# Layer 1's convolution as sums over tap rows by even and odd image rows

## The chip, the cores and the metric

The kernel runs on one core of one Trainium2 chip. A core has five engines with an instruction queue each: TensorE (PE; its weight loads are listed as PEld), VectorE (DVE), ScalarE (ACT), GpSimd (POOL) and SyncE (SP), which here only issues DMAs. Each engine works through its own queue in order; semaphores tie the queues together. The metric is the device time of one execution in microseconds, the median of several runs. One execution is also recorded by the hardware profiler; its trace is what is called the profile here.

## The reference: a hybrid of four layers

The input is x of 2 x 256 channels x 32 x 32, float32. Layer 0 is two Mamba blocks with normalisation, layer 1 a convolution with attention over a neighbourhood, layers 2 and 3 attention with experts. The change concerns layer 1:

```python
def _L1_conv_ref(x, w1, b1, w2, b2):
    k = lax.conv_general_dilated(x, w1, window_strides=(1, 1),
            padding=[(6, 6), (6, 6)], rhs_dilation=(2, 2), ...) + b1
    k = lax.conv_general_dilated(k, w2, ...) + b2          # 1x1, to 49 channels
    attn = softmax(k, axis=1)
    xp = pad(x, 6 on each side of both image axes)
    shifts = stack([xp[:, :, 2*u : 2*u + H, 2*v : 2*v + W] for u in 7 for v in 7])
    return einsum('bkchw,bkhw->bchw', shifts, attn)
```

So for each pixel 49 logits come from a 7 x 7 convolution with taps two pixels apart (tap row u and tap column v), followed by a 1 x 1 convolution; their softmax weighs the 49 shifted copies of x. Layer 0 ahead of it gives the x.

In layer 0 a Mamba block runs, for every image, 512 inner channels and 16 states n, the recurrence h = da * h + du * B along the 1024 pixels, and sums h * C over n.

## The kernel before

*Merged taps.* The 1 x 1 convolution follows the 7 x 7 one with nothing between, so the kernel multiplies the two weights once: `Taps.make` (from line 914) gives 7 x 7 taps of 256 channels x 49 outputs. It runs in 28 parts (tap row u, four of the 14 blocks "v, channel half" at a time), two steps each: PE transposes of w1 (`w1t`, line 939), an ACT copy, PE products with w2 (`taps_ps`, line 945), an ACT copy `taps_sb` (line 950), and a DMA of it on SP to a buffer in HBM. These steps are placed in the scans of layer 0, by `paced` (line 743): it hands out the steps of a list between given slots of a unit of scans, one slot for each scan.

*Layer 0's scans.* A unit of work is a chunk of 512 pixels of one image in one block: 2 images x 2 chunks x 2 blocks are eight units (`Mamba.scan`, line 546). In a unit, for each n = 0 to 15: SP loads `m_b` (line 599, four buffers), POOL makes m_h = m_du * m_b in two halves of 128 x 1024 (line 607, in the trace under the helper's line 179; six buffers), ACT the exponential m_da (line 617), VectorE four scans in place in m_h (line 621), PE transposes the result into `m_ht` (lines 575 and 577), and VectorE (line 591, `m_ya`) or ACT (line 589, `m_s`) multiplies it with C and gathers. Beside this the next unit's input products, `m_conv`, `m_delta`, `m_du` and so on are worked off in the slots. POOL's elementwise operations go through `Net.lined` (line 174), which chains each to the one before, so POOL works them off in the order in which the program emits them. The other engines' instructions are ordered by a scheduler.

*The convolution.* Sixteen output rows of 32 pixels fill one PSUM bank (512 float32 a partition). `Taps.convolve` (line 987) makes four passes, u = 3, 0, 1, 2; a pass takes tap rows u and u + 4 side by side as a weight block of 98 outputs (`Taps.load`, line 971; for u = 3, which has no partner, POOL sets the other half to zero). Since tap row u + 4 belongs to image rows eight below, the sums of both halves are kept eight (in pixels of one row phase: four) rows apart, in 35 rows over three banks, and the shift is undone when the logits of the 98 partitions are added, by two small products (line 1110). For each of seven v, two channel halves and each bank: one matmul of up to 512 columns, line 1001. 154 of them make an image; in the trace each float32 matmul is two instructions, so 308. `Taps.read` (line 1009) takes the banks with one ACT and one VectorE operation each into `lg`.

*Where it runs.* Image 0 (`early` in `layer0`, from line 861): two banks' steps lie in the slots of the last unit of layer 0 (slots 3 to 63), the third bank's follow its scans, beside layer 0's last products and norm. Image 1 (`layer1`, line 1031): `both` (line 757) takes two steps of the convolution and then one of a chain: turning image 0 (`turn`), weighing it (`weigh`: softmax, the band matrices, line 1126 on, and their products), and turning image 1.

Of the kernel before, what the change touches and what calls it, by code (L numbers as in the profile page):

```python
# [10 lines left out]
F32 = mybir.dt.float32  # L11
# [8 lines left out]
P = 128  # L20
NB = 2
HW = 1024
W = 32
# [742 lines left out]
def layer0(net, x, x_dram, m1, m2, load_image, taps, conv_dram, lg):  # L766
# [5 lines left out]
    with (  # L772
# [45 lines left out]
        for u, (m, j) in enumerate(units):  # L818
# [38 lines left out]
            if u + 1 < len(units):  # L857
                more = not u
                for n, first, end in ((2, 12, 32), (4, 35, 47), (3, 58, 63)):
                    steps += [(islice(aside, n + more), n + more, first, end)]  # L860
            else:
                last.close()
                m.ps_da = last.enter_context(tc.tile_pool(name="m_da2", bufs=2, space=PSUM))
                ps_acc = last.enter_context(tc.tile_pool(name="m_acc", bufs=1, space=PSUM))

                def place(u):
                    pool, tag, w = {
                        3: (one, "pre", TC + 3), 0: (two, "xs", TC), 1: (two, "delta", TC),
                        2: (two, "du", TC),
                    }[u]  # L870
                    a = pool.tile(
                        [P, NDC, w], F32, tag=tag, name=f"early_{u}",
                        bufs=3 if tag == "xs" else None,
                    )
                    return taps.load(u, a.rearrange("p d t -> p (d t)"))

                pair = {u: place(u) for u in taps.ORDER}
                def early():
                    for k in range(2):
                        a = ps_acc.tile([P, TC], F32, tag="acc", name=f"early_acc{k}")  # L880
                        acc = {k: taps.bank(a)}
                        yield from taps.convolve(0, pair, acc)
                        taps.read(acc, lg)

                steps += [(early(), 112, 3, 63)]
            own = m.back(j, u + 1 == len(units), u + 2 < len(units))
            if u + 1 == len(units):

# [5 lines left out]
        for _ in islice(done[0], 2):  # L894
            pass
        net.line = None
        acc = {2: taps.bank(ps_ht.tile([P, TC], F32, tag="ht", name="early_acc2"))}
        both(taps.convolve(0, pair, acc), done[0], 3)
        taps.read(acc, lg)


class Taps:
# [3 lines left out]
    def __init__(self, net, pool, keep, x, w1, w2):  # L906
# [4 lines left out]
        self.w2_sb = pool.tile([P, NTAP], F32, tag="w2", name="w2_sb", bufs=1)  # L911
        nc.scalar.dma_start(self.w2_sb, w2)

    def make(self, psum, dram):

        net, nc, pool = self.net, self.net.nc, self.pool
        self.made = [dram.tile([P, 14, NTAP], F32, name=f"taps_{u}") for u in range(7)]
        parts = [(u, k) for u in range(7) for k in range(0, 14, 4)]
        loaded = []

        def load():
# [5 lines left out]
            )  # L927
            loaded.append(w)

        load()  # L930
        load()
        for i, (u, k) in enumerate(parts):
            if len(loaded) < len(parts):
                load()
            w = loaded[i]
            n = min(4, 14 - k)
            ps = psum.tile([P, TC], F32, tag="mm", name=f"w1t_{u}_{k}")
            for a in range(n):
                nc.tensor.transpose(ps[:, a * P : (a + 1) * P], w[:, a, :], net.ident)
            wt = pool.tile([P, TC], F32, tag="w1t", name=f"w1ts_{u}_{k}", bufs=1)  # L940
            nc.scalar.copy(wt[:, : n * P], ps[:, : n * P])
            yield
            ps = psum.tile([P, TC], F32, tag="mm", name=f"taps_ps_{u}_{k}")
            for a in range(n):
                nc.tensor.matmul(
                    ps[:, a * NTAP : (a + 1) * NTAP], lhsT=wt[:, a * P : (a + 1) * P],
                    rhs=self.w2_sb, start=True, stop=True,
                )
            out = pool.tile([P, 4, NTAP], F32, tag="taps", name=f"taps_sb_{u}_{k}", bufs=3)
            nc.scalar.copy(  # L950
                out[:, :n, :], ps[:, : n * NTAP].rearrange("p (i t) -> p i t", t=NTAP)
            )
            nc.sync.dma_start(self.made[u][:, k : k + n, :], out[:, :n, :])
            yield


# [9 lines left out]
        nc.vector.tensor_copy(self.bias[:NTAP, :], ps[:NTAP, 0:1])  # L966
        yield

    ORDER = (3, 0, 1, 2)

    def load(self, u, flat):

        nc = self.net.nc
        w = flat[:, : 28 * NTAP].rearrange("p (a k t) -> p a k t", k=2, t=NTAP)
        if u == 3:
            nc.gpsimd.memset(w[:, :, 1, :], 0.0)
        for k in range(2):
            if u + 4 * k < 7:
                nc.sync.dma_start(w[:, :, k, :], self.made[u + 4 * k])
        return w.rearrange("p a k t -> p a (k t)")  # L980

    @staticmethod
    def bank(tile):

        return tile[: 2 * NTAP, :].rearrange("p (r c) -> p r c", c=W)

    def convolve(self, b, pair, acc):

        nc = self.net.nc
        for u in self.ORDER:  # L990
            r0 = 6 - 2 * u

            for v in (3, 0, 1, 2, 4, 5, 6):
                ci, co = max(0, 2 * v - 6), max(0, 6 - 2 * v)
                n = W - abs(2 * v - 6)
                for kc in range(NCC):
                    lhsT = pair[u][:, v * NCC + kc, :]
                    for k, a in acc.items():
                        lo, hi = max(16 * k, r0), min(16 * k + 16, r0 + W)
                        if lo < hi:  # L1000
                            nc.tensor.matmul(  # L1001
                                a[:, lo - 16 * k : hi - 16 * k, co : co + n], lhsT=lhsT,
                                rhs=self.x[:, kc, b, lo - r0 : hi - r0, ci : ci + n],
                                start=(u == (0 if k == 2 else 3) and v == 3 and kc == 0),
                                stop=(u == 2 and v == 6 and kc == NCC - 1),
                            )
                    yield

    def read(self, acc, lg):

        nc = self.net.nc
        for k, bank in acc.items():
            rows = 3 if k == 2 else 8
            src = bank.rearrange("m (r a) (h c) -> m a r c h", a=2, c=2)
            for a in range(2):
                to, at = lg[:, a, 8 * k : 8 * k + rows], src[:, a, :rows]
                if a:
                    nc.vector.tensor_scalar_add(to, at, self.bias)  # L1018
                else:
                    nc.scalar.activation(to, at, AF.Identity, bias=self.bias)  # L1020
            if k == 2:
                nc.gpsimd.memset(lg[:, :, 19], 0.0)

    @staticmethod
    def logits(tile):
        return tile[: 2 * NTAP, : 40 * W].rearrange(
            "m (a r c h) -> m a r c h", a=2, r=20, c=2
        )


def layer1(ctx, net, x, t, taps, lg0):
# [12 lines left out]
    one = ctx.enter_context(tc.tile_pool(name="c_one", bufs=1, side="right"))  # L1044
    two = ctx.enter_context(tc.tile_pool(name="c_two", bufs=2, side="right"))
    with (
        tc.tile_pool(name="c_pair", bufs=4) as pairs,
        tc.tile_pool(name="c_acc", bufs=1, space=PSUM) as ps_acc,
        tc.tile_pool(name="c_ps", bufs=1, space=PSUM) as ps2,
    ):  # L1050
        pair = {
            u: taps.load(u, pairs.tile([P, 28 * NTAP], F32, tag="pair", name=f"pair_{u}"))
            for u in taps.ORDER
        }
        lg, xk = {0: lg0}, {}

        def convolve(b):
            acc = {
                k: taps.bank(ps_acc.tile([P, TC], F32, tag=f"acc{k}", name=f"acc{k}"))
                for k in range(3)  # L1060
            }
            yield from taps.convolve(b, pair, acc)
            lg[b] = taps.logits(taps.keep.tile([P, 40 * W], F32, tag="lg", name=f"lg{b}"))
            taps.read(acc, lg[b])
            yield

        eye = one.tile([P, H + 6], F32, name="eye")
        nc.vector.memset(eye, 0.0)  # L1070
# [32 lines left out]
        def weigh(b, psum, tag):  # L1103

            att = one.tile([P, per, NTAP], F32, name=f"att{b}")
            for q in range(per):
                ps = psum.tile([P, TC], F32, tag=tag, name=f"lg_{b}_{q}", bufs=2)
                for k in range(2):
                    r = q % 4 * 4 + 4 * k
                    nc.tensor.matmul(  # L1110
                        ps[:, :NTAP],
                        lhsT=lg[b][:, q // 4, r : r + 4].rearrange("m r c h -> m (r c h)"),
                        rhs=net.ident[: 2 * NTAP, k * NTAP : (k + 1) * NTAP],
                        start=(k == 0), stop=(k == 1),
                    )
                nc.vector.tensor_copy(att[:, q, :], ps[:, :NTAP])
                if q % 4 == 3:
                    yield
# [46 lines left out]
                nc.vector.tensor_copy(t[:, b * per + q, :], ops[:, :C])  # L1165
            yield

        both(convolve(1), chain(turn(0), weigh(0, ps2, "a"), turn(1)), 2)
    return lambda psum, tag: weigh(1, psum, tag)


# [969 lines left out]
def conv_attn_hybrid(ctx: ExitStack, tc: tile.TileContext, a: dict, out: bass.AP):  # L2141
    nc = tc.nc
    net = Net(ctx, tc, a["cols"], a["rows"])
    main = ctx.enter_context(tc.tile_pool(name="main", bufs=1))
    lg = Taps.logits(main.tile([P, 40 * W], F32, tag="lg", name="lg0"))
    image = ExitStack()
    x = image.enter_context(tc.tile_pool(name="image", bufs=1, side="right")).tile(
        [P, NCC, NB, HW], F32, name="x"
# [159 lines left out]
```

## Time and profile before

| | us |
|---|---|
| median of 3 runs | 2045.58 |
| lowest and highest | 2043.87 and 2050.39 |
| profiled execution | 2050.42 |
| its span | 2048.7 |
| mean granted clock of TensorE | 0.961 |

The time splits so (bounds of the units found from the first scan of each):

| stretch | from | to | length |
|---|---|---|---|
| units 1 to 6 of layer 0's scans (unit 0 is first) | 165.5 | 876.8 | 711.3 |
| unit 7, with image 0's convolution | 876.8 | 1014.3 | 137.5 |
| layer 0's end | 1014.3 | 1056.2 | 41.9 |
| image 1's convolution in layer 1 | 1056.2 | 1165.5 | 109.3 |
| the rest: weighing of image 1, layers 2 and 3 | 1165.5 | 2048.7 | 883.2 |

How to read the rows: a group's row gives line, engine, operation, output and input tiles (names without numbers), shapes and count; then the busy time, the mean duration of one in ns; then the idle time of the engine just before them with what ended most of it. A row of windows gives the busy time and count on PE, PEld, VectorE, ScalarE and POOL, the granted clock (1.00 is full speed), the DMA share and GB/s. A row of the timeline gives start, length, engine, line, operation, tiles and how many were merged, in brackets what the engine waited for. Over the whole span the engines are busy like this:

```profile
PE 1874.6 (92%) x9938; PEld 1344.7 (66%) x9938; DVE 1332.1 (65%) x2138; ACT 946.9 (46%) x1713; POOL 1074.4 (52%) x729
```

The parts of `make` lie in units 0 to 5 (the copies from 86.0 to 751.8) and touch, in the trace, line 945's PE row (196 products, 26.9 us) and line 950's ACT row (28 copies, mean 0.32 us for the wide ones).

### The profile page before, as it was taken

The page shows a single profiled execution, that of the slowest core. Times are in us where ns is not written, and L with a number is a line of the kernel's source. Part 1 is how long each engine was busy: PE and PEld are TensorE (multiplying, and loading weights), DVE is VectorE, ACT ScalarE, POOL GpSimd, SP SyncE. Part 2 cuts the span into 40 slices and gives each one's busy share as a digit, 9 for nine tenths or more (in the row PEclk, how much of TensorE's full clock was granted, in tenths as well). Part 3 has the DMA queues.
Part 4 walks back from the last instruction along what each step waited for, and adds up shares of the span by engine and source line. Part 5 has one row for each costly group of instructions (what it writes and reads, how often), then busy time and mean ns, then how long its engine had stood idle before and what let it go on. Part 6 is the DMA issues. An engine that isn't in the chain of part 4 may idle for free. (4 is left out here: it accounts for less than half of the span.)

```text
span 2048.7 us, 27882 instructions
## 1 busy us (share of the span) xinstructions
PE 1874.6 (92%) x9938; PEld 1344.7 (66%) x9938; DVE 1332.1 (65%) x2138; ACT 946.9 (46%) x1713; POOL 1074.4 (52%) x729
## 2 busy tenths in 40 slices
PE   8788988988898988899999989999999899999995
PEld 3355665656565665655666555568999666799994
DVE  5889898998989989898614285774222445652223
ACT  4777877777877767674302253322111122221111
POOL 7788896978979698975404250012333200033330
PEclk9889999999999999799999999999999999999997
DMA  4334344343435334362130100046999400359995
GB/s 150 97 91 116 87 122 135 78 122 82 132 90 141 82 86 111 86 140 63 31 57 1 52 0 1 32 186 247 326 322 332 168 21 21 142 197 320 328 324 186
DMA packets 98857, 271.78 MB, mean 133 GB/s; under 512 B 35916, under 2 KB 54225, under 8 KB 82325
## 3 DMA queue, kind: packets, MB, share of 16 engines
q1 hardware_dynamic: 81268, 198.03, 29.1%
q0 software_dynamic: 14432, 68.31, 13.5%
q10 hardware_dynamic: 3008, 3.55, 0.5%
q8 instruction: 83, 1.36, 0.3%
q14 instruction: 66, 0.53, 0.1%
HBM read 200.80 MB, written 22.77 MB: 109 GB/s over the span
## 5 line engine op out<-in xcount | busy, mean ns | idle before, releaser
L179 POOL TENSOR_TENSOR m_h<-m_du,m_b 128x1024 f32<-128x1024 f32 x253 | 602.8, 2471 | 149.8 <-PE m_ht L577 73.5
L617 ACT ACTIVATE m_da<-m_delta,m_aneg 128x512 f32<-128x512 f32 x512 | 349.2, 694 | 153.2 <-DVE m_h L621 144.1
L621 DVE TENSOR_TENSOR_SCAN m_h<-m_da,m_state,m_h 128x512 f32<-128x512 f32 x256 | 314.0, 1266 | 22.0 <-POOL m_h L179 13.6
L577 PEld LDWEIGHTS m_ht<-ident,m_h 128*128 128x128 f32 x1600 | 193.5, 146 | 193.3 <-issue 64.2
L621 DVE TENSOR_TENSOR_SCAN m_h<-m_da,m_h 128x512 f32<-128x512 f32 x256 | 299.3, 1205 | 21.6 <-ACT m_da L617 16.5
L577 PE MATMUL m_ht<-ident,m_h 128*128 128x128 f32 x1600 | 254.1, 286 | 59.5 <-DVE m_h L621 28.4
L591 DVE SCALAR_TENSOR_TENSOR m_ya<-m_ht,m_ct,m_ya 128x512 f32<-128x512 f32 x324 | 231.3, 732 | 58.6 <-PE m_ht L577 49.6
L2067 PEld LDWEIGHTS h<-xts,we_l_late 128*128 128x128 f32 x2048 | 239.0, 193 | 10.6 <-issue 6.0
L2067 PE MATMUL h<-xts,we_l_late 128*128 128x128 f32 x2048 | 241.3, 276 | 4.6 <-DMA we_l_late<-in_l_experts_dram 1.9
L2075 DVE TENSOR_TENSOR hid<-hid,h 128x512 f32<-128x512 f32 x79 | 54.2, 686 | 236.6 <-PE h L2067 232.5
L1806 POOL DMA_INDIRECT x_l_early<-l_zs,l_source x15 | 17.8, 1187 | 339.1 <-ACT pt L1570 138.6
L2074 ACT ACTIVATE hid<-h 128x512 f32<-128x512 f32 x79 | 47.1, 597 | 315.7 <-PE h L2067 315.7
L575 PE MATMUL m_ht<-ident,m_h 128*128 128x128 f32 x896 | 140.5, 306 | 29.5 <-ACT m_s L589 13.4
L575 PEld LDWEIGHTS m_ht<-ident,m_h 128*128 128x128 f32 x896 | 124.3, 212 | 52.5 <-DVE m_h L621 16.8
L1806 POOL DMA_INDIRECT x_l_late<-l_zd,source x64 | 65.4, 1023 | 149.4 <-PE xt L2050 145.3
L2082 PE MATMUL o<-we_l_late,hid 128*128 128x256 f32 x512 | 122.7, 381 | 4.1 <-DVE y L2087 2.8
L430 PE MATMUL m_conv<-m_pre,m_taps 128*128 128x512 f32 x240 | 117.7, 609 | 5.8 <-ACT m_xs L436 3.4
L2089 POOL DMA_INDIRECT l_yd<-y,target x64 | 65.4, 1022 | 106.3 <-DVE y L2087 94.4
L589 ACT ACTIVATE m_s<-m_ht,m_ct 128x512 f32<-128x512 f32 x156 | 104.5, 686 | 31.8 <-DMA m_yb<-m_s 15.8
L2082 PEld LDWEIGHTS o<-we_l_late,hid 128*128 128x128 f32 x512 | 91.8, 190 | 15.3 <-DVE y L2087 3.9
L1001 PE MATMUL early_acc<-x,early 128*98 128x448 f32 (+24 forms) x308 | 98.6, 446 | 0.4 <-DVE lg L1018 0.4
L1001 PE MATMUL acc<-x,pair 128*98 128x416 f32 (+21 forms) x308 | 94.6, 455 | 0.0
(412 smaller groups left out, 3128.0 us busy)
## 6 DMA issues: line engine op xcount, KB each, us to landing
we_l_late<-in_l_experts_dram SPq DMA_DIRECT2D x64, 1536.0 KB, 9.5
m_yb<-m_s POOLq DMA_DIRECT2D x39, 1024.0 KB, 8.5
m_b<-m_bd SPq DMA_DIRECT2D x128, 256.0 KB, 3.5
we_l_early<-in_l_experts_dram SPq DMA_DIRECT2D x15, 1536.0 KB, 8.2
m_ya<-m_yb POOLq DMA_DIRECT2D x7, 1024.0 KB, 8.8
w<-in_l_w_dram SPq DMA_DIRECT2D x21, 256.0 KB, 6.1
l_yl<-l_yd SPq DMA_DIRECT2D x8, 512.0 KB, 10.7
l_zd<-l_z SPq DMA_DIRECT2D x7, 512.0 KB, 3.3
```

The costliest lines, as they stand in the source:

```text
L179: self.line = do(*args, **named)
L430: nc.tensor.matmul(ps, lhsT=self.taps[:, dc * 4 + k, :], rhs=pre[:, dc, k : k + TC], start=(k == 0), stop=(k == 3),)
L575: nc.tensor.matmul(a, lhsT=h, rhs=net.ident, start=True, stop=True)
L577: nc.tensor.transpose(a, h, net.ident)
L589: nc.scalar.activation(to[:, i, :], ps, AF.Copy, scale=c)
L591: nc.vector.scalar_tensor_tensor(ya[:, i, :], ps, c, ya[:, i, :], ALU.mult, ALU.add)
L617: net.decayed = nc.scalar.activation(da, delta[:, dc, :], AF.Exp, scale=self.aneg[:, i : i + 1])
L621: nc.vector.tensor_tensor_scan(h, da, h, 0.0 if first else state[:, n, dc : dc + 1], ALU.mult, ALU.add)
L1001: nc.tensor.matmul(a[:, lo - 16 * k : hi - 16 * k, co : co + n], lhsT=lhsT, rhs=self.x[:, kc, b, lo - r0 : hi - r0, ci : ci + n], start=(u ...
L1806: nc.gpsimd.indirect_dma_start(out=x, out_offset=None, in_=rows[:, :], in_offset=bass.IndirectOffsetOnAxis(ap=source[:, g : g + 1], axis=0 ...
L2067: nc.tensor.matmul(ps[:, at], lhsT=w12[:, s, kc, at], rhs=xt[:, kc * P : (kc + 1) * P], start=(kc == 0), stop=(kc == NCC - 1),)
L2082: gate.o = nc.tensor.matmul(ps[:, :C], lhsT=ht[:, mc * P : (mc + 1) * P], rhs=w[:, 8 + mc, :], start=(mc == 0), stop=(mc == NHC - 1),)
```

## The change

With taps two rows apart, an output row of one row phase reads input rows of the same phase only. Call s the row pair within a phase's even or odd half: the rows of a phase are split once more into even ones and odd ones. The seven tap rows are then a filter of odd and even taps over even and odd rows, a filter of length 7 over two half-rate sequences. The change computes it with three sums, a scheme in which one sum is shared by both halves:

- sum 0 runs on (even + odd rows added, the new tile `both`, made by POOL in two 128 x 512 additions) with tap rows 3, 1 and 5;
- sum 1 runs on odd rows with the tap differences 6-5, 4-3, 2-1 and 0;
- sum 2 runs on even rows with 2-3, 0-1, 6 and 4-5;
- even output rows are sum 0 + sum 1, odd ones sum 0 + sum 2 (with the bias in sums 1 and 2).

Each sum covers half the image's rows, so it fits one bank. There are 113 matmuls an image instead of 154; a sum goes through 28 or 29 steps and its bank is then read: sums 1 and 2 by one ACT and one VectorE operation, sum 0 by four VectorE additions into `lg`.

What else moves:
- `make` has 24 new POOL subtractions (`less`, through `lined`), one after each part with u > 0, from two neighbouring copies; one buffer. Its parts run with u as the inner loop. SP writes 44 pieces instead of 28, of 196 bytes per block where two are side by side.
- The taps are kept in pairs (a to f) and loaded with 6 contiguous loads instead of 7; the zero half is gone.
- In `layer0`: the early pairs lie in other buffers (d, c, e, f; a and b together in "pre"), the three early sums share one bank one after the other, 67 of the 87 steps lie in slots 5 to 63 and the last 20 after the scans, one to each step of layer 0's end.
- In `layer1`: three steps of the convolution to one of the chain; all tap pairs have a buffer of their own; `lg` has 36 instead of 40 rows.

The core of the diff:

```diff
+    PAIRS = {
+        "a": ("3", "1"), "b": ("5",), "c": ("6-5", "4-3"), "d": ("2-1", "0"),
+        "e": ("2-3", "0-1"), "f": ("6", "4-5"),
+    }
+    SUMS = (
+        (1, (("d", -1, 1, 8, 0), ("c", 0, 0, 1, 1), ("c", 1, 0, 7, 0))),
+        (2, (("e", 0, 0, 8, 0), ("f", 1, 0, 1, 1), ("f", 2, 0, 6, 0))),
+        (0, (("a", 0, 0, 8, 0), ("b", 1, 0, 7, 0))),
+    )
+    STEPS = 3 * (7 * NCC * 2 + 1)
...
-        parts = [(u, k) for u in range(7) for k in range(0, 14, 4)]
+        parts = [(u, k) for k in range(0, 14, 4) for u in range(7)]
...
+        def keep(name, tile, k, n):
+            if name in home:
+                pair, i = home[name]
+                nc.sync.dma_start(self.made[pair][:, k : k + n, i, :], tile[:, :n, :])
...
-            nc.sync.dma_start(self.made[u][:, k : k + n, :], out[:, :n, :])
+            keep(f"{u}", out, k, n)
+            if u:
+                less = pool.tile([P, 4, NTAP], F32, tag="less", name=f"less_{u}_{k}", bufs=1)
+                x, y = (past, out) if u % 2 else (out, past)
+                net.lined(nc.gpsimd.tensor_sub, less[:, :n, :], x[:, :n, :], y[:, :n, :])
+                keep(f"{u - 1}-{u}" if u % 2 else f"{u}-{u - 1}", less, k, n)
             yield
...
+    def added(self, b, both):
+        rows = self.x[:, :, b].rearrange("p k (s e a) w -> p k e s a w", e=2, a=2)
+        for kc in range(NCC):
+            self.net.lined(
+                self.net.nc.gpsimd.tensor_add, both[:, kc],
+                rows[:, kc, 0], rows[:, kc, 1],
+            )
+    def convolve(self, b, pair, both, bank, lg):
         nc = self.net.nc
+        rows = self.x[:, :, b].rearrange("p k (s e a) w -> p k e s a w", e=2, a=2)
+        for which, passes in self.SUMS:
+            acc = bank(which)
+            if which == 2:
+                self.added(b, both)
+            src = both if which == 0 else rows[:, :, which % 2]
             for v in (3, 0, 1, 2, 4, 5, 6):
                 ci, co = max(0, 2 * v - 6), max(0, 6 - 2 * v)
                 n = W - abs(2 * v - 6)
                 for kc in range(NCC):
+                    first = v == 3 and kc == 0
+                    todo = list(passes if which or first else passes[::-1])
+                    if first and which == 1:
+                        todo[1:] = ("c", 1, 0, 1, 0), ("c", 1, 1, 7, 0), passes[1]
+                    for i, (name, rho, lo, hi, edge) in enumerate(todo):
+                        w = pair[name][:, v * NCC + kc]
+                        w = w[:, 1, :] if edge else w.rearrange("p k t -> p (k t)")
+                        nc.tensor.matmul(
+                            acc[: w.shape[1], lo:hi, :, co : co + n], lhsT=w,
+                            rhs=src[:, kc, lo + rho : hi + rho, :, ci : ci + n],
+                            start=first and i == 0,
+                            stop=v == 6 and kc == NCC - 1 and i + 1 == len(todo),
+                        )
+                        if i in (0, len(todo) - 1):
+                            yield
+            self.read(which, acc, lg)
+            yield
...
-                steps += [(early(), 112, 3, 63)]
+                early = early()
+                many = Taps.STEPS - 20
+                steps += [(islice(early, many), many, 5, 63)]
...
-        acc = {2: taps.bank(ps_ht.tile([P, TC], F32, tag="ht", name="early_acc2"))}
-        both(taps.convolve(0, pair, acc), done[0], 3)
-        taps.read(acc, lg)
+        both(early, done[0], 1)
...
-        both(convolve(1), chain(turn(0), weigh(0, ps2, "a"), turn(1)), 2)
+        both(convolve(1), chain(turn(0), weigh(0, ps2, "a"), turn(1)), 3)
```

## The prediction

> **What bounds the kernel now.** I read the page first (busy shares and slices), then the windows of layer 0's units and of layer 1, then the timeline of the stretches the change touches. One execution was profiled: 2050.42 us, of which 2048.7 are the span, so 1.7 lie around it; it stands 4.8 above the median of 2045.58. All sums below are made against 2050.4 and carried to the median at the end. A shift of 0.3%, 6 us, is about the least a measurement of this kernel can tell from none.
>
> From the page:
> ```profile
> L179 POOL TENSOR_TENSOR m_h<-m_du,m_b 128x1024 f32<-128x1024 f32 x253 | 602.8, 2471 | 149.8 <-PE m_ht L577 73.5
> L621 DVE TENSOR_TENSOR_SCAN m_h<-m_da,m_state,m_h 128x512 f32<-128x512 f32 x256 | 314.0, 1266 | 22.0 <-POOL m_h L179 13.6
> L1001 PE MATMUL early_acc<-x,early 128*98 128x448 f32 (+24 forms) x308 | 98.6, 446 | 0.4 <-DVE lg L1018 0.4
> L1001 PE MATMUL acc<-x,pair 128*98 128x416 f32 (+21 forms) x308 | 94.6, 455 | 0.0
> ```
> The convolution (line 1001) is some 95 us of TensorE per image. In the scans, POOL's m_h idles 149.8 us, half of it for m_ht to free its buffers: POOL runs ahead of VectorE, whose scans wait for POOL only 13.6 us here. That lead is what the change spends.
>
> Windows (PE, PEld, DVE, ACT, POOL busy; granted clock): two ordinary units of layer 0, the last unit with image 0's convolution, its tail, and layer 1:
> ```profile
> 282.20:399.80 117.60, 104.16 (x541) 69.45 (x542) 105.81 (x120) 93.40 (x172) 98.84 (x50) 0.97 0.44 118
> 399.80:517.30 117.50, 105.07 (x541) 71.50 (x539) 107.24 (x119) 89.52 (x142) 100.67 (x51) 0.96 0.41 102
> 876.80:1014.30 137.50, 133.53 (x571) 77.57 (x570) 109.16 (x121) 71.59 (x106) 83.32 (x44) 1.00 0.35 80
> 1014.30:1056.20 41.90, 39.55 (x245) 30.78 (x243) 13.43 (x43) 5.00 (x13) 7.47 (x23) 0.98 0.17 32
> 1056.20:1165.50 109.30, 107.43 (x419) 61.32 (x419) 29.44 (x62) 19.56 (x56) 36.63 (x57) 0.98 0.10 15
> ```
> An ordinary unit is VectorE's (106-107 of 117.5 us), with PE and POOL close behind. The last unit is TensorE's: 133.5 of 137.5, 20 us longer than the others with no more VectorE work. Layer 1 is TensorE's too, 107.4 of 109.3. In the last unit even POOL waits for the transposes (timeline):
> ```profile
> 984.45 4.65 POOL L179 TENSOR_TENSOR m_h<-m_du,m_b 128x1024 f32<-128x1024 f32 x2 [8.54 <-PE m_ht L577]
> 999.46 4.69 POOL L179 TENSOR_TENSOR m_h<-m_du,m_b 128x1024 f32<-128x1024 f32 x2 [10.36 <-PE m_ht L577]
> ```
>
> **What the Trainium skill says.** "TensorE: Matmul & The Clock Gate", Back-to-back issue gap, lets streamed matmuls cost by their columns, with an issue floor for small ones. The trace agrees in kind, not in size: here the f32 matmul is two instructions, and each has a higher price and floor:
> ```profile
> 1141.86 3.70 PE L1001 MATMUL acc<-x,pair 128*98 128x448 f32 x12
> 1145.62 3.09 PE L1001 MATMUL acc<-x,pair 128*98 128x364 f32 x12
> 1045.57 3.70 PE L1001 MATMUL early_acc<-x,early 128*98 128x120 f32 x40
> ```
> The first two differ by 0.61 us for 12 x 56 mean columns (the shape named is one of those merged). Starts of 448-column instructions lie 0.373 us apart, so 0.833 ns a column, 1.667 ns for both instructions. The third gives 92 ns for a small one.
> "GPSIMD Engine Reference", Elementwise, puts a two-input f32 operation at about 2.6 cycles an element plus dispatch. Here 512 elements took 1.27 us and 1024 took 2.36, so 2.13 ns an element and 0.18 fixed: 0.60 us for 196 elements, 0.39 for 98. The trace's slope is used.
> "DMA: Bandwidth & Descriptors", Why small descriptors are slow, names a fixed cost per packet. The old tap loads (196-byte pieces, 343 KB) landed in 5.2-5.9 us where a 1024 KB load took 7.5. The new ones are contiguous and not on the path longer than before.
>
> **The change part by part.**
> *TensorE columns.* Before: four passes of 32 rows x 200 columns (the widths of the seven taps v summed) x 2 channel halves = 51,200 columns, of which 800 are 14 small matmuls. (50,400 x 1.667 ns) + 14 x 0.184 = 86.6 us. After: 11,200 + 11,200 + 12,000 = 34,400 in full ones and 28 edge matmuls of 52-64 columns: 57.3 + 5.2 = 62.5. So **-24.1 us of TensorE per image**.
> *Layer 1 (image 1).* TensorE bound, so -24.1, less what comes up late: the weighing of image 0 (per q four POOL band steps of 0.68 and 1.9 of VectorE) gets a period of about 3.8 us instead of 4.6, +1.5 (0 to 6); the first sum wants a double tap tile (686 KB instead of 343), +0.7; four VectorE additions instead of one read before the logits, +0.8. **-21** (-15 to -23). POOL's sum of even and odd rows, 2 x 1.27 us, is done during the second sum.
> *Last unit (image 0).* 46,400 columns (77.8 us) lie in its scans now. After it is 67 of 87 steps, 22,400 columns in full and 28 edges: 37.3 + 5.2 + the 4,712 of the third sum's first steps, 7.9 = 50.4, so 27.4 us less of PE: 133.5 becomes 106, just under VectorE's 109. The unit then should last as the others do, 117.5: -20 (-14 to -23). Two bank switches within the scans (the three sums share one bank, so the next sum's first matmul waits for two reads of about 0.45, with the transposes queued behind it on PE) +1. In the tail 7,288 columns instead of 4,800 follow the last transposes, of which some 1,600 fill the wait of the last norm that small matmuls fill now, and 800 end beside the transposes mm_t: +2.4. **-16.6** (-10 to -20). The zero half's memset (0.68 us of POOL, twice) goes; the POOL had time.
> *The 24 subtractions.* 18 x 0.60 + 6 x 0.39 = 13 us of POOL in units 0 to 5, where POOL has 98-103 of some 117.5. That would hide by sums. But these go through `lined`, which keeps POOL in the order of emission, and each waits for ScalarE's copy of the taps, which waits for taps_ps on PE, behind m_ht. What is queued behind it on POOL are the m_h (and often the m_du) that the next scans need. One site in the timeline of before:
> ```profile
> 276.08 2.37 POOL L179 TENSOR_TENSOR m_du<-m_delta,m_xs 128x1024 f32<-128x1024 f32 x1
> 278.41 4.70 POOL L179 TENSOR_TENSOR m_h<-m_du,m_b 128x1024 f32<-128x1024 f32 x2
> 280.73 0.99 PE L945 MATMUL taps_ps<-w_sb,w1ts 128*128 128x49 f32 x8
> 281.76 0.32 ACT L950 COPY taps_sb<-taps_ps 128x196 f32<-128x196 f32 x1
> 282.15 1.19 DVE L621 TENSOR_TENSOR_SCAN m_h<-m_da,m_h 128x512 f32<-128x512 f32 x1
> ```
> In the changed order the subtraction stands ahead of that m_du and the first m_h. The copy ends at 282.08; + 0.60 + 2.37 + 2.35 = 287.4, where the scan started at 282.15. It is 5.2 late, of which VectorE can fill about 1.5 with two m_ya of 0.73 that the new order puts ahead. So I went through all 24 with the copies' times of before: five at unit borders cost about 4 each (20), five at n = 10 about 3 each (15), two at n = 15 about 3 (6), the others together 3: **44 gross**. Some 10 of it takes the place of VectorE's idle time that units have at n = 10 and 11 already (1.68 + 1.41 + 1.16 us in the second one above, and the like), and I take 7 off for later waits for m_ht that a delayed scan no longer meets. **+27** for the units. Bounds: +5 if the scheduler's order lets the copies come earlier relative to the scans or VectorE fills the gaps; +55 if no idle time absorbs anything and POOL, its lead lost, becomes the bound of the stretch n = 10 to 15 (49 us of POOL there against 44 of VectorE).
> *SP.* 44 tap writes instead of 28, each behind its copy or subtraction; m_b is loaded some four n ahead and lands in 3.5 us, so 0 (up to +3 where it waits behind one). ScalarE and VectorE get nothing else in the scans but the reads: ScalarE loses one of three per image, VectorE gains three of about 0.45 us; counted above.
>
> Sum: -21 - 16.6 + 27 = -10.6, 2039.8 for the profiled execution, **2035** at the median.
>
> **The rivals.**
> (A) The subtractions hide: VectorE's scans keep their times since POOL's idle time of some 17 us a unit takes the wait. Penalty +5 to +12: about 2010-2020. For it: POOL idles for m_ht, so it is ahead on average. Against: the copies end 5-18 us after the m_h before them, which is more than the lead.
> (B) Slower: POOL's order decides. One mechanism: each subtraction holds up POOL at the place in its line, and every late m_h is paid by the scans in full. From 44 us on (1.8 us for each of the 24) the kernel is slower by more than the 6; with +55 it is 2045.6 + 17 = 2063. For it: gross 44 already, and the border sites have m_du behind them too. Against: VectorE has 10 us of idle per unit that can be used up.
> (C) The gain is half hidden: VectorE at 109 and the chain of weighing hold the last unit and layer 1 up, 24 instead of 37.6 gained, with +27: about 2048, no change. Against: VectorE has 29 of 109 us in layer 1.
>
> **How the numbers follow.** Forecast with its own range 2027-2042: 0.37. A: 0.17. B: 0.34. C: 0.12. The range from 2013 to 2066 leaves out the best half of A and the worst of B. Faster by over 6 us: 0.34 of the forecast's and A, 0.50; within: 0.03 and most of C, 0.14; slower: B and a little of C, 0.36.
>
> **What would show it.** Line 1001's group near 62 us per image; layer 1's conv about 88 us long; the last unit near 118; in units 0 to 5 idle time of the scans put down to POOL m_h rising from 13.6 to some 40, and POOL's subtractions waiting for taps_sb. If the units keep 117.5, A holds; if they go beyond 125, B. The forecast would be wrong altogether if the last unit stayed near 137, since then PE was not its bound.

## The result, and the profile after

The changed kernel takes 2125.12 us (median of 4, 2114.55 to 2130.18) against 2044.82 for the kernel before; the ratio is 1.0371, 95% interval 1.0343 to 1.0399. It is slower by about 80 us where 10 less were forecast. The profiled execution took 2123.78 us, 2122.1 of it the span. Stage by stage, from the two traces (a unit begins with its first scan):

| stage | before | after | change | predicted |
|---|---|---|---|---|
| up to the first scan | 42.7 | 43.9 | +1.2 | 0 |
| units 0 to 5 | 710.0 | 794.6 | +84.6 | +27 |
| unit 6 | 124.1 | 121.3 | -2.8 | 0 |
| unit 7, with image 0's convolution | 137.5 | 128.9 | -8.6 | -19 |
| from its last scan to image 1's first matmul | 41.9 | 47.4 | +5.5 | +3.1 |
| from there to image 1's logits | 109.6 | 99.1 | -10.5 | -21.7 |
| the rest | 882.9 | 886.9 | +4.0 | 0 |
| span | 2048.7 | 2122.1 | +73.4 | -10.6 |

So two things went wrong. The units in which the taps are made lost three times what was priced. And the two stages with the convolution each brought about half of what was expected, so that, with the stretch between them, 13.6 us were gained instead of 37.6.

Four rows of the page of the kernel after (groups: busy us, mean ns, then the idle time before them and its main releaser):

```profile
L179 POOL TENSOR_TENSOR m_h<-m_du,m_b 128x1024 f32<-128x1024 f32 x253 | 603.7, 2484 | 71.3 <-PE m_ht L577 29.9
L621 DVE TENSOR_TENSOR_SCAN m_h<-m_da,m_h 128x512 f32<-128x512 f32 x256 | 298.9, 1206 | 59.2 <-POOL m_h L179 33.3
L589 ACT ACTIVATE m_s<-m_ht,m_ct 128x512 f32<-128x512 f32 x156 | 104.8, 685 | 59.7 <-DMA m_yb<-m_s 40.6
L179 POOL TENSOR_TENSOR less<-taps_sb,taps_sb 128x196 f32<-128x196 f32 (+1 forms) x24 | 13.7, 571 | 150.7 <-ACT taps_sb L977 135.7
```

The 24 subtractions are 13.7 us of work, as priced (13), but POOL stood idle 150.7 us ahead of them. The idle time of m_h, POOL's lead, fell from 149.8 to 71.3 us, and the scans now wait for POOL (the second row's idle time was 21.6 before, most of it for ScalarE). The third row has no term in the prediction: ScalarE's m_s waits 40.6 us for a DMA, 15.8 before. That is the second way of the loss, below.

Windows of the same kernel (PE, PEld, VectorE, ScalarE, POOL busy; granted clock): units 2, 3 and 7, the stretch up to image 1's first matmul, and image 1's convolution:

```profile
301.00:437.20 136.20, 116.13 (x545) 77.17 (x546) 105.36 (x118) 93.98 (x172) 102.36 (x54) 0.89 0.40 100
437.20:576.30 139.10, 118.08 (x549) 76.17 (x547) 110.58 (x120) 90.52 (x139) 102.65 (x56) 0.90 0.36 88
959.80:1088.70 128.90, 120.91 (x553) 69.53 (x551) 109.86 (x123) 72.18 (x107) 88.46 (x47) 0.97 0.34 89
1088.70:1136.10 47.40, 43.68 (x187) 24.93 (x188) 14.20 (x44) 5.42 (x14) 9.15 (x28) 0.94 0.17 65
1136.10:1234.10 98.00, 95.63 (x332) 44.42 (x331) 29.88 (x65) 19.28 (x55) 35.14 (x51) 0.94 0.04 13
```

In units 2 and 3 VectorE and POOL are busy within 4 us of before, but the units take 18 to 22 us more. TensorE is busy 12 to 13 us longer with nearly the same count of instructions, at a mean granted clock of 0.89 to 0.90 instead of 0.96 to 0.97. Over units 0 to 5 its busy time went from 619.5 to 669.4 us and its clock from 0.945 to 0.899. The last unit is still 120.9 us of TensorE where 106 were predicted.

### The profile page after: what moved, and what is told of

Its sections match the earlier page's. It is cut to its first block, busy times and chain, and to the rows that moved or that the text cites. A ratio compares the mean times of both kernels' runs of the same rounds, so it can differ in the third digit from the quotient of the medians.

```text
span 2122.1 us, 27589 instructions
## 1 busy us (share of the span) xinstructions
PE 1903.7 (90%) x9774; PEld 1338.0 (63%) x9774; DVE 1340.7 (63%) x2144; ACT 948.9 (45%) x1711; POOL 1089.2 (51%) x755
## 3 DMA queue, kind: packets, MB, share of 16 engines
q8 instruction: 82, 1.34, 0.2%
## 5 line engine op out<-in xcount | busy, mean ns | idle before, releaser
L179 POOL TENSOR_TENSOR m_h<-m_du,m_b 128x1024 f32<-128x1024 f32 x253 | 603.7, 2484 | 71.3 <-PE m_ht L577 29.9
L577 PEld LDWEIGHTS m_ht<-ident,m_h 128*128 128x128 f32 x1600 | 199.3, 150 | 254.5 <-DVE m_h L621 89.3
L577 PE MATMUL m_ht<-ident,m_h 128*128 128x128 f32 x1600 | 271.6, 294 | 93.5 <-DVE m_h L621 56.0
L2108 PEld LDWEIGHTS h<-xts,we_l_late 128*128 128x128 f32 x2048 | 239.7, 193 | 10.5 <-issue 5.7
L575 PE MATMUL m_ht<-ident,m_h 128*128 128x128 f32 x896 | 147.8, 316 | 40.0 <-ACT m_s L589 19.2
L575 PEld LDWEIGHTS m_ht<-ident,m_h 128*128 128x128 f32 x896 | 130.4, 221 | 63.1 <-DVE m_h L621 22.7
L589 ACT ACTIVATE m_s<-m_ht,m_ct 128x512 f32<-128x512 f32 x156 | 104.8, 685 | 59.7 <-DMA m_yb<-m_s 40.6
L430 PE MATMUL m_conv<-m_pre,m_taps 128*128 128x512 f32 x240 | 124.0, 635 | 2.7 <-ACT m_pre L405 2.4
L2123 PEld LDWEIGHTS o<-we_l_late,hid 128*128 128x128 f32 x512 | 91.8, 190 | 15.3 <-DVE y L2128 3.9
L179 POOL TENSOR_TENSOR less<-taps_sb,taps_sb 128x196 f32<-128x196 f32 (+1 forms) x24 | 13.7, 571 | 150.7 <-ACT taps_sb L977 135.7
L700 PE MATMUL m_out<-m_out_sb,m_xs 128*128 128x256 f32 x256 | 81.4, 441 | 0.0
## 6 DMA issues: line engine op xcount, KB each, us to landing
l_yl<-l_yd SPq DMA_DIRECT2D x8, 512.0 KB, 11.2
```

What stands on the lines that cost most here:

```text
L179: self.line = do(*args, **named)
L430: nc.tensor.matmul(ps, lhsT=self.taps[:, dc * 4 + k, :], rhs=pre[:, dc, k : k + TC], start=(k == 0), stop=(k == 3),)
L575: nc.tensor.matmul(a, lhsT=h, rhs=net.ident, start=True, stop=True)
L577: nc.tensor.transpose(a, h, net.ident)
L589: nc.scalar.activation(to[:, i, :], ps, AF.Copy, scale=c)
L2108: nc.tensor.matmul(ps[:, at], lhsT=w12[:, s, kc, at], rhs=xt[:, kc * P : (kc + 1) * P], start=(kc == 0), stop=(kc == NCC - 1),)
```

## The experiments

Three theories: W, the subtractions' place in POOL's line makes POOL wait; P, the work they add on POOL; S, the other edits to the taps' making (44 writes, new order of the parts). The measure is the length of units 0 to 5: 710.0 us before, 794.6 after. Five profiled executions with the same taps' making (two of the two-steps-later kernel below, one each of the kernels called grouped, best and grouped_48) lie between 719.7 and 721.6, so some 2 us are noise; the kernel before was profiled once.

### Without the subtractions, and with subtractions that wait for nothing

```diff
-                net.lined(nc.gpsimd.tensor_sub, less[:, :n, :], x[:, :n, :], y[:, :n, :])
-                keep(f"{u - 1}-{u}" if u % 2 else f"{u}-{u - 1}", less, k, n)
+                keep(f"{u - 1}-{u}" if u % 2 else f"{u}-{u - 1}", out, k, n)
```

> The changed kernel without the 24 subtractions: the pieces that would hold differences are written from the copies themselves, so the convolution's taps are other numbers; everything else, the 44 writes and the order of the parts included, is as in the changed kernel. Theory W (each subtraction makes POOL's line wait for ScalarE's copy, and VectorE and TensorE then wait for POOL): units 0 to 5 fall from 794.6 us together to about 710-720, the time to 2035-2050. Theory P (the 13.7 us of added work on POOL): the same here. Theory S (the writes on SP and the new order of the parts slow the units): stays at 2115-2130.

For the second one the operands are two blocks of the identity matrix, `net.ident[:, s : s + NTAP]` broadcast over the tile, in the same place.

> The changed kernel with the 24 subtractions at the same places in POOL's line and of the same size, but of two constant blocks instead of the copies, so none waits for ScalarE; the differences of the taps are left out. W: as without them but for a few us of POOL work, 2035-2055. P: stays at 2110-2130. S: stays too.

Units 0 to 5 took 716.7 and 719.8 us. So S costs 6.7 us, P 3.1 (little more than the noise), and all the rest of the 84.6, 74.8 us, goes when the subtractions don't wait for their copies: W. The times themselves, 2101.72 and 2107.58 us, missed every expectation, for a reason that has nothing to do with the units: other taps give other logits, and other tokens for the experts. The group of x_l_late has 70 loads instead of 64 in both, and the part after image 1's logits took 943 to 945 us instead of 883, some 60 more. A kernel with a data-dependent end can only be compared by its stages when numbers are left out.

### The subtraction one and two steps later

```diff
+                def differ(u=u, k=k, n=n, past=past, out=out):
+                    less = pool.tile(...)
+                    ...
+                    net.lined(nc.gpsimd.tensor_sub, less[:, :n, :], x[:, :n, :], y[:, :n, :])
+                    keep(..., less, k, n)
+                wait = differ
             yield
```

`wait()` is called at the next step of `make`, or at the one after it.

> The changed kernel with each subtraction, and the write of its result, emitted one step of the taps' making later than its copies, so that the copy is some 4 to 20 us old when POOL comes to it. W: most of the loss goes, 2045-2070, with POOL's waits for taps_sb down from 135.7 us to below 50. P and S: 2110-2130.

> The same, two steps later. W: no wait for taps_sb of any size, 2035-2055, and TensorE's granted clock in units 0 to 5 back from 0.90 to about 0.96. P and S: 2110-2130.

One step later: 2067.97 us, units 748.7, POOL's waits for taps_sb 49.9 us. Two steps later: 2040.39 us beside 2043.11 for the kernel before on the same chip, units 719.7 (719.9 in a second execution, further down), waits 4.6 us. Both as W expects. The waits view (us in total, times, longest) of the kernel after and of the two-steps-later one:

```profile
POOL less L179 <- ACT taps_sb L977: 135.7, 14, 14.4
POOL less L179 <- ACT taps_sb L980: 4.6, 1, 4.6
```

With the waits gone TensorE's busy time over the six units is back as well (618.9 us), and its clock (0.953), so the lower clock in the changed kernel came with them.

### Which sites cost what

Only some subtractions stay in their place; the others are two steps late:

```diff
+                if (u, k) in IN_PLACE:
+                    differ()
+                else:
+                    wait = differ
```

> The two-steps-later kernel, but the six subtractions at the borders of units (five borders) stand at the places of the changed kernel. The prediction priced these at 20 us. Theory A (the waits are paid site by site and add up): units 0 to 5 take 719.7 + 20 to 35 = 740-755 us, the granted clock near 0.96. Theory F (a wait leaves TensorE idle, its clock is lowered, and the taps and m_ht behind it come later still, so that many waits together cost more than the sum): these alone cost little, 722-735, and only all 24 together the 75.

> The same with only the five subtractions at n = 10 at the places of the changed kernel. The prediction priced them at 15 us gross, 8 or so after idle time that VectorE had. A: 719.7 + 10 to 25 = 730-745; border's and this one's excess together with some 15 for the other 13 sites make the 75. F: 720-727, and the two together far below 75.

Border: 739.8 us, 20.1 above the two-steps-later kernel, the very sum that the prediction had for these sites (20), though it counted five of them and the run has six, at three of which POOL waited. Ten: 751.8, 32.1 above it, where 15 were priced gross. Both are more than theory F allows, border at the foot of A's range and ten above it. The two make 52.2 of 74.9, so most of the loss is paid without all 24 waiting together. By difference 22.7 are left for the other 13 subtractions, which were priced at 9. They weren't run alone, so whether the rest adds up site by site is not shown.

The two groups do their harm in different ways. Against the two-steps-later kernel, the scans' waits for m_h rose in border from 15.3 to 29.7 us and ScalarE's for the DMA m_yb<-m_s only from 13.3 to 14.9. In ten the scans' waits rose only to 18.7, but ScalarE's to 26.6, and those of VectorE's m_ya for m_ht from 52.9 to 70.0. Of ten's 32 us, 23 come from units 3 and 5, with one site each. The timeline of unit 3 in that run shows why they are so dear:

```profile
485.17 0.60 POOL L179 TENSOR_TENSOR less<-taps_sb,taps_sb 128x196 f32<-128x196 f32 x1 [15.89 <-ACT taps_sb L983]
485.73 4.66 POOL L179 TENSOR_TENSOR m_h<-m_du,m_b 128x1024 f32<-128x1024 f32 x2
490.33 0.87 POOL L179 DMA_DIRECT2D m_yb<-m_s  x1
...
500.09 1.84 ACT L589 ACTIVATE m_s<-m_ht,m_ct 128x512 f32<-128x512 f32 x3 [4.46 <-DMA m_yb<-m_s]
...
500.83 1.80 PE L577 MATMUL m_ht<-ident,m_h 128*128 128x128 f32 x8 [3.38 <-ACT m_s L589]
...
502.66 0.75 DVE L591 SCALAR_TENSOR_TENSOR m_ya<-m_ht,m_ct,m_ya 128x512 f32<-128x512 f32 x1 [4.24 <-PE m_ht L577]
```

Read it downwards. POOL waits 15.89 us for the copy; that makes the two m_h late, which the prediction counted. But POOL's line also issues the DMA m_yb<-m_s, and that is late too: issued at 490.33, it frees its source 9.8 us later, at 500.09. There is one m_s buffer, so ScalarE waits (4.46), then TensorE for ScalarE (3.38), then VectorE for TensorE (4.24). The stall comes twice, the second time a whole n after the subtraction.

### The DMA alone, late

```diff
-    LATER = 3
+    LATER = 4
```

> The two-steps-later kernel with the DMAs m_yb<-m_s, which POOL issues from the same line, emitted one n later (LATER 4 instead of 3), everything else as it was: this delays only the DMAs, by some 7 us each, and no m_h. Theory D (a late DMA on POOL's line is dear by itself, since ScalarE's next m_s needs the one buffer that it empties, and m_ht and VectorE's m_ya wait behind): ScalarE's wait for m_yb<-m_s grows from 13 us to over 60 and units 0 to 5 from 719.7 to 760-830. Theory M (only late m_h cost time): 715-730.

Units 0 to 5: 751.1 us, 31.4 above the two-steps-later kernel; 2080.88 us in all. The row of the waits view (us in total, times, longest), in the two-steps-later kernel and in this one:

```profile
ACT m_s L589 <- DMA m_yb<-m_s: 13.3, 6, 3.6
ACT m_s L589 <- DMA m_yb<-m_s: 75.7, 25, 5.5
```

With every m_h at its old place in POOL's order, a later DMA alone costs 31 us (POOL's waits for taps_sb, which rose from 4.6 to 15.6 us here, may have a part in it). That is less than the 40 that theory D named as the least, and well above M's 730: D holds, in a smaller size.

### The output width of the matmuls

The other half of the miss. First the timeline of TensorE in image 1's convolution, of the kernel after; the row of four has the two instructions of an edge (49 outputs) and the two of the wide matmul behind it:

```profile
1150.85 0.82 PE L1041 MATMUL acc<-x,pair_d 128*98 128x392 f32 x2
1151.60 1.13 PE L1041 MATMUL acc<-x,pair_c 128*49 128x56 f32 x4
1152.57 0.82 PE L1041 MATMUL acc<-x,pair_d 128*98 128x392 f32 x2
```

Then the same place in the timeline of the kernel with the matmuls grouped by width, where no edge stands between:

```profile
1071.46 0.82 PE L1057 MATMUL acc<-x,pair_d 128*98 128x392 f32 x2
1072.12 0.82 PE L1057 MATMUL acc<-x,pair_c 128*98 128x392 f32 x2
1072.78 0.49 PE L1057 MATMUL acc<-x,pair_d 128*98 128x392 f32 x1
```

From one pair_d to the next it is 1.72 us with an edge matmul between and 1.32 without, so an edge costs 0.40 us, not the 0.184 of the prediction. In sum 0 pairs a (98 outputs) and b (49) alternate and no edge is there; in the kernel after:

```profile
1211.45 0.86 PE L1041 MATMUL acc<-both,pair_a 128*98 128x416 f32 x2
1212.24 0.81 PE L1041 MATMUL acc<-both,pair_b 128*49 128x364 f32 x2
1212.99 0.94 PE L1041 MATMUL acc<-both,pair_a 128*98 128x416 f32 x2
```

From one a to the next it is 1.54 us, where 416 + 364 columns at 1.667 ns are 1.30. Both say 0.22 to 0.24 us for going from 98 outputs to 49 and back, and since no matmul of sum 0 is short, it isn't the shortness of the edges that costs it. What in TensorE causes it is not shown. The regrouped kernel writes all of a sum's 49-wide matmuls in one row after its first step:

```diff
+            small = [t for t in todo if t[2][4] or t[2][0] == "b"]
+            todo = [t for t in todo if t not in small]
+            todo = todo[:at] + small + todo[at:]
```

> The two-steps-later kernel with the convolution's matmuls of one sum in another order: all that write 49 outputs (the edges, and pair b) in one row behind the first step, not between those that write 98. Same matmuls, same result. Theory T (each change of the output width, there and back, costs TensorE about 0.22 us beyond the columns, 42 times an image): the convolution of image 1 gets 8-9 us shorter, line 1041's group in the last unit by 5-7, the time 12-16 us below the two-steps-later kernel's 2040, so 2024-2028. Theory N (small matmuls are dear by themselves, wherever they stand): no change, 2040.

The convolution's busy time (line 1041's group in the kernel after) fell from 78.7 to 70.0 us for image 1 and from 80.4 to 74.3 for image 0 (the two-steps-later kernel against this one). That is theory T, in the size expected: N, which allowed no change, is out. The time is 2035.74 us, a ratio to the kernel before of 0.9949 (0.9932 to 0.9965).

> The two-steps-later kernel again, timed in rounds: 2036-2042, a ratio of 0.996-0.999 to the kernel before; the subtractions' waits were what made the change slower, and the rest of it gains less than the 37.6 us predicted: about 10 in the last unit, 6 in layer 1.

It took 2045.2 us, 1.002 (0.9999 to 1.0041): no gain that can be measured, a miss by half a per cent. So with the waits gone and the widths mixed the scheme is worth nothing, and grouping the widths is worth 0.7% (from 1.002 to 0.9949, each against the kernel before on its own chip), what was expected of it. The 2024 to 2028 started from 2040, a single execution below the 2045.2 of this median.

### Two edits that brought nothing

```diff
+            do = self.net.nc.vector if b else self.net.nc.gpsimd
+            self.net.lined(do.tensor_add, both[:, kc], rows[:, kc, 0], rows[:, kc, 1])
```

> The grouped kernel with image 1's sum of even and odd rows on VectorE instead of POOL, where it stands ahead of the copies xs that the first transposes of layer 1 wait for. If POOL's line is what delays the start of image 1's convolution (9.4 us after image 0's ends, 5.8 before the change), it is 2-3 us faster than the grouped one; if the tap load sets the start (its landing 4.0 us after the issue), no change.

2037.79 us, 0.996 (0.9945 to 0.9975): as the grouped kernel. Image 1's first matmul came 11.2 us after image 0's last transposes, not earlier than 10.5. The tap load, which landed 4.0 us after its issue, wasn't the limit either. In that trace the eight pairs of transposes of turn(0), most of them waiting for their POOL copy, stand ahead of the convolution in TensorE's queue.

```diff
-                steps += [(islice(early, many), many, 5, 63)]
+                steps += [(islice(early, many), many, 5, 48)]
```

> The grouped kernel with the convolution of image 0 put into slots 5 to 48 of the last unit instead of 5 to 63. If the last unit does not get shorter than 129-131 us because its last 30 us stay bound by TensorE (m_g, m_out, m_ht and an even share of the convolution there) while the saved time lies idle in its first 90, the unit falls to 119-124 and the time by 6-10 us against the grouped kernel, to 2026-2030. If VectorE (110 us busy) or POOL sets it, no change.

2035.08 us, 0.9951 (0.9931 to 0.9971): no change, and the unit got longer, 145.4 us against 130.5, while the stages behind it got shorter by as much. From the first scan of unit 7 to image 1's logits it is 266.2 us, 267.4 in the grouped kernel. Work moved between stages; what TensorE has to do in all of them stayed.

### The subtraction out of the line

```diff
-                net.lined(nc.gpsimd.tensor_sub, less[:, :n, :], x[:, :n, :], y[:, :n, :])
+                nc.gpsimd.tensor_sub(less[:, :n, :], x[:, :n, :], y[:, :n, :])
```

> The changed kernel with the matmuls grouped, and with the subtractions emitted where the change has them but without `lined`, so that the scheduler may put them anywhere in POOL's queue; it puts them 2 to 6 POOL operations later. Theory W with additive waits: units 0 to 5 take 712-728 us as with the steps put off by hand, and the time is that of the grouped kernel, 2030-2038, ratio to the kernel before 0.993-0.998. If only a copy two steps old is old enough, the units stay above 740.

Units 726.6 us, 2036.15 us in all, 0.9953 (0.9931 to 0.9975). Leaving one word out, so that the scheduler may place the subtraction behind POOL's next m_h and DMA, does what the steps put off by hand did, to within 7 us of the units.

## Why the prediction was wrong

The mechanism was the right one, but the likeliest case was given the wrong size; the outcome is rival B ("POOL's order decides", every late m_h paid by the scans in full), and beyond its 2063 by 62 us. By the prediction's own sign for B, units beyond 125 us, it is B too: units 0 to 5 took 132 on average.

*The 24 subtractions, +27.* The step that failed, by its size:

| term | priced | measured |
|---|---|---|
| at the unit borders (priced as five, six in the run) | 20 | 20.1 |
| five at n = 10 | 15 | 32.1 |
| the other 13 | 9 | 22.7, by difference |
| taken off for VectorE's idle time and later waits | -17 | not seen |
| 44 writes, order of the parts | 0 | 6.7 |
| POOL's 13 us of work | 0 | 3.1 |
| sum | 27 | 84.7 |

The measured column must close, since one of its terms was found by difference. What was measured apart says enough: the border sites cost their gross price with nothing taken off, and those at n = 10 twice theirs. For the latter only the m_h behind the subtraction was priced, not the DMA m_yb<-m_s that POOL issues from the same line; nor has the bound of +55 a term for it. How the 32.1 divide between the two was not measured.

*The clock.* Not in the prediction. TensorE was busy 50 us longer in units 0 to 5. Its mean clock there was 0.945 in the kernel before, in that without subtractions and in that with constants in them, 0.953 with all of them two steps late, 0.938 in border, 0.930 in ten, 0.927 with the late DMA and 0.899 in the kernel after. How much of the 75 us it made, and how much of its slower work only filled time that was idle anyway, stays open; that two groups of sites make 52.2 of it speaks against a large part that appears only when all wait together.

The Trainium skill, "TensorE: Matmul & The Clock Gate", HAM oscillation, says that idle gaps of TensorE above about 3.4 us bring its clock down. Windows of ten's unit 3, around the wait of 3.38 us in the timeline above, and of unit 3 of the kernel after:

```profile
497.60:501.10 3.50, 0.27 (x2) 0.28 (x3) 0.83 (x1) 1.01 (x2) 3.42 (x3) 0.99 0.52 110
501.10:511.30 10.20, 10.20 (x28) 6.06 (x26) 3.52 (x6) 6.66 (x12) 10.12 (x5) 0.50 0.08 27
519.40:522.80 3.40, 1.34 (x9) 0.99 (x9) 3.40 (x4) 2.57 (x4) 3.40 (x3) 1.00 0.30 79
522.80:543.30 20.50, 20.50 (x54) 12.73 (x54) 9.62 (x12) 9.54 (x16) 20.42 (x11) 0.50 0.41 89
```

In ten the trace agrees: behind the wait the clock is 0.50 for 10.2 us. In the kernel after one such gap wasn't needed: TensorE was busy 1.34 of 3.40 us, in pieces with waits of at most 0.85, and then had half its clock for 20.5 us. So a wait slows TensorE for a time after it too: in ten the late DMA did so for 10.2 us.

*TensorE columns, -24.1 per image.* The columns were right and the changes of width left out. The price of 0.092 us an instruction came from a row of 52 to 120 columns in which all matmuls had 98 outputs; between wide ones an edge costs 0.40 us. With 28 edges and 14 changes between a and b it is 42 x 0.22 = 9.2 us an image. Once grouped, the busy time is 24.6 (94.6 to 70.0) and 24.3 (98.6 to 74.3) us below the kernel before.

*Last unit, -20, and layer 1, -21.* From unit 7's first scan to image 1's logits the changed kernel gained 13.6 us (289.0 to 275.4) where 37.6 were forecast, the grouped one 21.6. So about 8 of the missing 24 are the widths. Of the 16 that the grouped kernel still misses, 12.0 are in the last unit (7.0 gained instead of 19), 0.5 in the stretch behind it and 3.5 in image 1's convolution.

In the last unit the convolution's own time on TensorE fell by 25.2 us (84.8 to 59.6), close to the 27.4 priced. But the rest of TensorE's work there was busy 56.5 us instead of 48.7, so the grouped kernel's unit has 116.1 us of TensorE, not 106. It didn't fall to the 117.5 of the others but lasts 130.5, with VectorE busy 110.0; what holds it up stays open. In the stretch behind it, image 1's first matmul comes 10.8 us after image 0's last transposes instead of 5.8 (10.5 in the grouped kernel), where only 0.7 was priced for the larger load. And after this gap image 1's convolution starts at a lower clock than before (windows of the kernels before and after):

```profile
1056.20:1066.10 9.90, 9.90 (x20) 3.93 (x20) 0.00 (x0) 0.37 (x1) 0.39 (x2) 0.74 1.10 160
1136.10:1146.00 9.90, 9.90 (x34) 6.43 (x33) 1.25 (x6) 0.00 (x0) 0.00 (x0) 0.50 0.33 127
```

That is about 2.4 us of work at full speed, an estimate (9.9 x (0.74 - 0.50)); in the grouped kernel the clock of these 9.9 us is 0.53. The waits of the weighing are small: TensorE is idle 3.9 us in the grouped kernel's stretch, 1.9 before, where 1.5 was taken.

*What held:* the page's sign of it (scans waiting for POOL: 51.6 us by the waits view, 16.9 before), the 13 us of POOL, the site worked out in the prediction. In the kernel after, its copy ended at 295.68, the two-step arithmetic gives 301.0, and the scan started at 301.03 after a wait of 3.25 us, where about 3.7 had been worked out.

## What to carry to other kernels

A small operation put into an in-order queue costs not its own time but its wait, passed on to everything behind it in that queue, and DMAs issued from the queue are part of that: follow each to the buffer it frees. Put such an operation where its input is old, or leave its place to the scheduler. When the matmuls of a sum have two output widths, keep those of one width together.

## What the runs showed of the hardware

- Going from float32 matmuls of 98 outputs to ones of 49 and back cost TensorE 0.22 to 0.24 us: an edge 0.40 us instead of 0.184, a step of pairs a and b 1.54 us instead of the 1.30 of its columns. Between pairs of one width it was not seen (1.32 us for 784 columns, 1.31 by the columns).
- The DMAs m_yb<-m_s issued one n later (about 7 us, a unit of 117 us having 16), with POOL's order of the m_h unchanged, lengthened units 0 to 5 by 31.4 us.
- After 3.4 us in which TensorE was busy only 0.27 or 1.34 us, its granted clock was 0.50 for 10.2 and 20.5 us; the second time no single wait was longer than 0.85 us.
- With the waits in place TensorE's mean granted clock over units 0 to 5 was 0.899 instead of 0.945, and it was busy 50 us longer with nearly the same instructions.
